# First expert's first half summed in two base tiles, z2d stored later, FFN2's rows loaded sooner, in a gated cross-attention and mixture-of-experts kernel

## The chip, the cores and the metric

The kernel runs on one core of a Trainium2 chip. The core has five engines, each with its own in-order instruction queue: TensorE (PE, matrix products), VectorE (DVE), ScalarE (ACT), GpSimd (POOL) and SyncE (SP), which here only issues DMA transfers. Transfers run on 16 DMA engines. A DMA instruction in a queue holds back everything behind it in that queue until what it waits for has happened. The metric is the device time of one execution in microseconds: 1840.61 us, median of 3 runs (1840.03 to 1844.49).

## The reference

There are B = 4 batches of 2048 tokens with 512 features, all in float32. Each batch has a context of 128 rows.

```python
n = layernorm(x)                                  # no affine
Q, K, V = n @ Wq + bq, ctx @ Wk + bk, ctx @ Wv + bv
attn = softmax(Q @ K.T) / sqrt(512)
x = x + tanh(g_x) * (attn @ V)
n = layernorm(x)
e = argmax(mean_tokens(n) @ Wr + br)              # one expert of 8 for each batch
h = relu(n @ W1[e] + b1[e])                       # 512 -> 2048
x = x + tanh(g_f) * (h @ W2[e] + b2[e])           # 2048 -> 512
```

## The kernel before

**Strassen products.** The two feed-forward products (FFN1 and FFN2) use the seven-product form of a 2 x 2 block product (as Winograd arranged it), FFN1 on two levels (7 outer groups of 7 inner products), FFN2 on one. This needs sums of blocks on both sides. The left sums of FFN1 are made from the normalised tokens in `z_prepare` (tiles z1 to z7, each with 7 places). The right sums are sums of the expert's weights. They are the same for all tokens of a batch and are called staging here.

**Staging.** An expert has two halves (`fh` 0 and 1) of its 2048 hidden features. For each half, `stage_w1` does two 128-row chunks `pc` of four outer blocks. It loads the four blocks with four inner blocks each (1 MB) from HBM into places 1 to 4 of a tile `base` ([128, 4, 7, 128]), makes three outer sums in a tile `tt` ([128, 3, 7, 128]) with `outer_sums` and the three inner sums of each outer block with `inner_sums`, all on POOL, four subtractions a call. The finished tiles are stored to HBM (W1d: one tensor for the four base blocks, one for the three tt blocks). `stage_w2` does the same for W2, on one level, in two chunks `kp`, in the same `base` buffer, and stores the four sums to W2d. `base` and `tt` have one buffer each (`stp`, one buffer). A store is not issued where its data is made: `later` queues it, and `settle` issues it some steps later, so that SP need not stand at it.

**Weights into PE.** `fetch` loads staged blocks from W1d, raw or summed blocks from W2 and W2d, into a ring of `NW` = 6 tiles `w` of 0.5 MB, in the order in which PE uses them. Before the change it asks `staged_upto` whether the whole half has been staged. FFN1's group i has a tile A (inner products 6, 1, 2, 7) and a tile B (3, 4, 5), and its last three products run inside the next group.

**Attention.** Tokens come in 16 blocks of 512. Each block is a generator, `attention`: load x and xT, statistics, scores, softmax, weighted values, statistics, store x1d (the first residual sum), normalise in place on ACT, transpose on PE, sum for routing, store z2d. The first nine blocks (numbered 0 to 8; 0 to 3 are batch 0) run in the head, a loop of steps in which every live generator emits one piece; block i starts at step `skew` x i. The tuple `AT_ONCE` gives how many steps a block waits at each of its lags. When block 1 ends, `z_prepare(0, 0)` joins the loop, and when block 3 ends, `first_expert`: `route` (mean, product with Wr, arg max; SP then reads the expert's number), then staging. The loop ends when blocks 0 to 7 are done and the first half's weights are staged. Then the main loop goes through batches, pairs of token blocks and halves: `ffn1`, then `ffn2`. `tick` emits the remaining attention and staging pieces between PE's products at rates set by `PACE`. The order on each engine is thus written by the program, not by a scheduler.

**FFN2.** `ffn2` has two half-passes `cp`, with 7 products of 3.45 us each. Product m3 accumulates in the bank that the sum of m5 is read from. That sum adds to the residual rows `xr`, which DVE has to have in SBUF: `load(cp)` reads them from x1d (`fh` 0) or y1d (`fh` 1), after the first product of the half-pass; they are written back to y1d or to the output. `xr1` and `xr0` have one buffer each.

**What is queued where.** All transfers of the head, of the ring and of staging are on SP's queue. x, x1d and z2d of the later attention blocks are on ACT's queue. Each transfer takes one of eight completion counters in turn, and so waits for the transfer eight places before it in program order. The lines of the profile that matter: L204 scores, L245 weighted values, L263 normalise, L278 transposes, L259 and L287 stores of x1d and z2d, L446 staging sums, L481 and L512 loads of W1 and W2, L471 stores of staged tiles, L563, L570 and L576 ring loads, L591 feed-forward products, L646, L662 and L666 z's load, second-level and first-level sums, L834 to L853 the xr rows.

Of the kernel before, what the change touches and what calls it, by code (L numbers as in the profile page):

```python
# [18 lines left out]
P = 128  # L19
# [70 lines left out]
def flamingo(tc, ctx, x, xT, cxT, g_x, g_f, WqT, Wk, Wv, bqk, bv, Wr, br, W1, b1, W2, b2, out):  # L90
# [52 lines left out]
    for b in range(B):  # L143
# [8 lines left out]
        for fh in range(2):  # L152
            for lo, n in ((0, 4), (4, 3)):
                t = dram.tile([P, n, 2, 7, P], F32, name=f"W1d_{b}{fh}{lo}")
                W1d.update({(b, fh, lo + i): (t, i) for i in range(n)})
            W2d[b, fh] = dram.tile([P, 2, 4, 2, Q], F32, name=f"W2d_{b}{fh}")
# [11 lines left out]
    def attention(b, blk, pools):  # L168
# [104 lines left out]
        for kc in range(KC + 1):  # L273
# [12 lines left out]
            yield  # L286
        queue.dma_start(z2d[b, blk], zT)  # L287
# [9 lines left out]
    AT_ONCE, LATER = (4, 2, 3, 7, 4, 5, 6), (2, 1, 3, 6, 3, 3, 8)  # L297
# [10 lines left out]
    if True:  # L308
# [7 lines left out]
        nc.sync.dma_start(w["k"], Wk)  # L316
# [137 lines left out]
    stores = []  # L454
    LOAD, AGE = (10, 6), 3

    def later(dst, src):

        stores.append([AGE, dst, src])

    def flush():
        for _, dst, src in stores:
            nc.sync.dma_start(dst, src)
        stores.clear()

    def older():
        for x in stores:
            x[0] -= 1
        while stores and stores[0][0] < 0:
            _, dst, src = stores.pop(0)  # L470
            nc.sync.dma_start(dst, src)  # L471

    def settle(n):
        for _ in range(n):
            older()
            yield

    def stage_w1(b, fh, eng):
        def load(pc):
            t = stp.tile([P, 4, 7, P], F32, tag="base", name="base")  # L480
            nc.sync.dma_start(  # L481
                t[:, :, 1:5, :],
                W1[bass.ds(expert[b][0], 1), fh, pc].rearrange("e p o i c -> p (e o) i c"),
            )
            return t

        flush()
        base = load(0)
        yield from settle(LOAD[b > 0])
        for pc in range(2):  # L490
            tt = stp.tile([P, 3, 7, P], F32, tag="tt", name="tt")
            for _ in outer_sums(
                eng, *(t[:, i, 1:5, :] for t, n in ((base, 4), (tt, 3)) for i in range(n))
            ):
                yield from settle(1)
            for src, lo in ((base, 0), (tt, 4)):
                for _ in inner_sums(eng, src):
                    yield from settle(1)
                later(W1d[b, fh, lo][0][:, :, pc], src)
            if pc == 0:  # L500
                yield from settle(1)
                base = load(1)
                yield from settle(LOAD[b > 0])
        yield from settle(AGE + 1)

    def stage_w2(b, fh, eng):
        for kp in range(2):
            flush()
            t = stp.tile([P, 4, 7, P], F32, tag="base", name="base2").rearrange(
                "p o i c -> p (o i c)"  # L510
            ).rearrange("p (o c) -> p o c", o=7)
            nc.sync.dma_start(  # L512
                t[:, 0:4, :],
                W2[bass.ds(expert[b][0], 1), fh, kp].rearrange("e p o k c -> p (e o) (k c)"),
            )
            yield from settle(LOAD[b > 0])
            for _ in outer_sums(eng, *(t[:, i, :] for i in range(7))):
                yield from settle(1)
            later(W2d[b, fh][:, kp].rearrange("p o k c -> p o (k c)"), t[:, 3:7, :])
            yield from settle(AGE + 1)  # L520
        flush()

    def stage(b, eng):
        for fh in range(2):
            yield from stage_w1(b, fh, eng)
            flush()
            staged_upto[0] += 1
            yield from stage_w2(b, fh, eng)
            staged_upto[0] += 1
# [6 lines left out]
    Wt, items, staged_upto = {}, [], [0]  # L536
# [14 lines left out]
    def fetch(freed=0):  # L551

        ring["freed"] += freed
        while ring["issued"] < min(ring["freed"] + NW, len(items)):
            st, kind, i = items[ring["issued"]]
            b, fh = st // (2 * NF), st % 2
            if 4 * b + 2 * fh + (kind == "2") >= staged_upto[0]:
                return
# [83 lines left out]
    def z_prepare(b, blk):  # L642
# [22 lines left out]
        def level1(o, l, r, op):  # L665
            nc.vector.tensor_tensor(z[o][:, 0:4, :], z[l][:, 0:4, :], z[r][:, 0:4, :], op)  # L666
# [30 lines left out]
    def s4(cp):  # L697
        hsum(h[12], h[12], h["s2"], ALU.subtract, cp)

    def ffn1(b, blk, fh):  # L700
# [46 lines left out]
        def group(i):  # L747
# [13 lines left out]
            def copied(v):  # L761
# [4 lines left out]
                t22 = s7p.tile([P, 2, Q], F32, tag="s722", name="s722")  # L766
# [13 lines left out]
            def summed(j, a, v):  # L780
# [6 lines left out]
                else:  # L787
                    c = cp_.tile([P, 2, Q], F32, tag="cg", name="cg", bufs=2)
# [12 lines left out]
        for i in range(8):  # L801
            cur = group(i) if i < 7 else None
            for k, (who, m) in enumerate((
# [8 lines left out]
                if i == 7 and k == 3:  # L812
                    s3(0)
            fetch((cur is not None) + (last is not None))
# [4 lines left out]
    def ffn2(b, blk, fh, half):  # L819
# [6 lines left out]
        xr, s7 = {}, {}  # L826

        def tokens(t, i, cp):
            return t[b, 2 * blk + i][:, 2 * cp : 2 * cp + 2, :]

        def load(cp):
            for i in (1, 0):
                xr[cp, i] = xrp.tile([P, 2, H], F32, tag=f"xr{i}", name="xr")
                nc.sync.dma_start(xr[cp, i], tokens(y1d if fh else x1d, i, cp))  # L834
# [7 lines left out]
        def store(cp, i):  # L842
# [4 lines left out]
            else:  # L847
                nc.sync.dma_start(tokens(y1d, i, cp), xr[cp, i])
# [32 lines left out]
        load(0)  # L881
        yield
        for cp in range(2):
# [4 lines left out]
            cur[6]()  # L888
            bias(cp, 1)
            yield  # L890
# [18 lines left out]
            if cp == 0:  # L909
                cur = group(1)  # L910
                load(1)
# [13 lines left out]
    def first_expert():  # L925
        yield from route(0, ps_k, "pk")
        yield from stage_w1(0, 0, nc.gpsimd)
        flush()
        staged_upto[0] += 1
        fetch()  # L930
        bias2_load(0)
        fetched[0] = 1
        yield from stage_w2(0, 0, nc.gpsimd)
        staged_upto[0] += 1
        yield from stage_w1(0, 1, nc.gpsimd)
        flush()
        staged_upto[0] += 1
        yield from stage_w2(0, 1, nc.gpsimd)
        staged_upto[0] += 1
# [3 lines left out]
    skew = 14  # L943
    step = 0
    while any(g is not None for g in streams[:-1]) or not fetched[0] or prep is not None:
        for i, g in enumerate(streams):
            if g is not None and step >= skew * i and next(g, StopIteration) is StopIteration:
# [3 lines left out]
                if i == 1:  # L951
                    prep = z_prepare(0, 0)
# [13 lines left out]
        if work is not None and next(work, StopIteration) is StopIteration:  # L966
            work = None
# [39 lines left out]
    PACE = {"slow": (0.6, 0.7, 0.7), "staged": (1.4, 0.7, 0.5, 0.5)}  # L1007
# [71 lines left out]
```

## Time and profile before

| What | Value |
|---|---|
| median of 3 runs | 1840.61 us |
| profiled execution | 1841.68 us, span 1839.9 us |
| mean granted PE clock | 0.966 |
| PE busy | 1713.2 us (93%) |
| DVE, ACT, POOL busy | 1025.3, 583.0, 679.3 us |
| DMA | 483.08 MB, 262 GB/s over the span |
| first weight load of the first expert issued | 149.56 us |
| first FFN1 product on PE | 221.26 us |
| first FFN2 product | 270.98 us |
| first product of the second half's FFN1 | 354.74 us |

The page divides the span in 40 slices of 46 us; a digit is the busy share of a slice in tenths, PEclk the clock that PE was granted. A row of waits names the engine and line that waited, what ended the wait, the sum in us, the number of times and the longest. A row of a timeline has the start, the duration, the engine, line and operation, output and inputs, and in brackets how long the engine had been idle and what ended it. SPq is SP's queue issuing a transfer; its duration is that of the issue, not of the transfer. Line numbers are those of the kernel before.

### The profile page before, as it was taken

The page shows a single profiled execution, that of the slowest core. Times are in us where ns is not written, and L with a number is a line of the kernel's source. Part 1 is how long each engine was busy: PE and PEld are TensorE (multiplying, and loading weights), DVE is VectorE, ACT ScalarE, POOL GpSimd, SP SyncE. Part 2 cuts the span into 40 slices and gives each one's busy share as a digit, 9 for nine tenths or more (in the row PEclk, how much of TensorE's full clock was granted, in tenths as well). Part 3 has the DMA queues.
Part 4 walks back from the last instruction along what each step waited for, and adds up shares of the span by engine and source line. Part 5 has one row for each costly group of instructions (what it writes and reads, how often), then busy time and mean ns, then how long its engine had stood idle before and what let it go on. Part 6 is the DMA issues. An engine that isn't in the chain of part 4 may idle for free.

```text
span 1839.9 us, 22357 instructions
## 1 busy us (share of the span) xinstructions
PE 1713.2 (93%) x7894; PEld 1448.4 (79%) x7894; DVE 1025.3 (56%) x1636; ACT 583.0 (32%) x1277; POOL 679.3 (37%) x616
## 2 busy tenths in 40 slices
PE   7977497899999999998999989999999999999998
PEld 5554286687878888787888878788888888888887
DVE  3586165466564866656464745465545564555453
ACT  1244250250523324161333315050505050505150
POOL 0136374285632393146510573266201510151010
PEclk9997698999999999999999999999999999999999
DMA  6485878799897888788867787879675757575754
GB/s 257 172 320 224 307 252 309 280 334 367 283 362 287 302 307 336 240 292 303 333 218 241 253 303 250 286 261 367 219 224 173 264 174 225 173 267 170 228 171 169
DMA packets 186589, 483.08 MB, mean 263 GB/s; under 512 B 13680, under 2 KB 42352, under 8 KB 173808
## 3 DMA queue, kind: packets, MB, share of 16 engines
q1 hardware_dynamic: 182592, 459.36, 71.2%
q10 hardware_dynamic: 3888, 22.31, 3.0%
q8 instruction: 63, 1.03, 0.2%
q14 instruction: 46, 0.38, 0.1%
HBM read 344.78 MB, written 136.84 MB: 262 GB/s over the span
## 4 chain that ended last, share of the span: by engine, by line
PE 70%; DMA 15%; DVE 8%; POOL 3%; issue 2%; ACT 1%; SPq 1%; ACTq 0%; DVEq 0%; POOLq 0%
PE Y L591 28%; PE X L591 18%; PE Q L591 17%; DMA z<-z2d 3%; PE psc L204 3%; DMA w<-W2d 2%; DMA base<-in_W_dram 2%; PE pav L245 2%; POOL base L446 2%; DVE xr L853 2%; DVE z L666 1%; DMA W2d<-base 1%; DMA W1d<-tt 1%; DMA out_dram<-xr 1%; POOL tt L446 1%
## 5 line engine op out<-in xcount | busy, mean ns | idle before, releaser
L591 PE MATMUL Y<-z,w 128*128 128x256 f32 x1344 | 334.5, 382 | 5.1 <-DVE c L785 2.2
L591 PEld LDWEIGHTS Y<-z,w 128*128 128x128 f32 x1344 | 251.7, 190 | 48.8 <-issue 5.9
L610 ACT COPY Y<-X 128x512 f32<-128x512 f32 x144 | 82.3, 571 | 563.8 <-PE X L591 563.4
L715 ACT ACTIVATE h<-c,b1T 128x256 f32<-128x256 f32 x512 | 229.7, 501 | 73.6 <-DVE c L731 33.0
L446 POOL TENSOR_TENSOR base<-base 128x512 f32<-128x512 f32 x144 | 190.7, 1333 | 147.6 <-DMA base<-in_W_dram 142.4
L591 PE MATMUL Q<-w,h 128*128 128x256 f32 x1024 | 238.1, 386 | 7.1 <-DMA w<-W2d 7.1
L591 PE MATMUL Y<-w,s 128*128 128x256 f32 x1024 | 235.3, 383 | 2.2 <-DMA w<-W2d 2.2
L591 PE MATMUL X<-w,h 128*128 128x256 f32 x1024 | 232.5, 379 | 0.0
L591 PE MATMUL X<-z,w 128*128 128x256 f32 x896 | 216.3, 380 | 14.5 <-DMA w<-W1d 14.5
L591 PEld LDWEIGHTS Q<-w,h 128*128 128x128 f32 x1024 | 197.7, 194 | 38.5 <-issue 10.8
L662 POOL TENSOR_TENSOR z<-z 128x256 f32<-128x256 f32 x224 | 188.4, 865 | 97.0 <-DMA z<-z2d 54.8
L591 PEld LDWEIGHTS Y<-w,s 128*128 128x128 f32 x1024 | 196.6, 192 | 32.4 <-issue 5.3
L591 PEld LDWEIGHTS X<-w,h 128*128 128x128 f32 x1024 | 194.3, 190 | 29.7 <-issue 3.3
L591 PE MATMUL Q<-z,w 128*128 128x256 f32 x896 | 216.5, 381 | 0.6
L591 PEld LDWEIGHTS X<-z,w 128*128 128x128 f32 x896 | 170.1, 191 | 38.6 <-issue 15.4
L591 PEld LDWEIGHTS Q<-z,w 128*128 128x128 f32 x896 | 169.6, 191 | 24.7 <-PE Y L591 1.0
L734 POOL TENSOR_TENSOR r<-r,cg 128x512 f32<-128x512 f32 x32 | 40.6, 1269 | 370.8 <-DVE cg L789 370.8
L591 PE MATMUL Y<-w,h 128*128 128x256 f32 x512 | 126.3, 401 | 24.7 <-DVE xr L853 24.7
L591 PEld LDWEIGHTS Y<-w,h 128*128 128x128 f32 x512 | 101.9, 202 | 45.4 <-DVE xr L853 29.8
L195 POOL TENSOR_TENSOR rstd<-ve,mhalf 128x4 f32<-128x4 f32 x32 | 32.8, 1025 | 230.6 <-DVE ve L194 218.3
L853 DVE SCALAR_TENSOR_TENSOR xr<-X,gf,xr 128x512 f32<-128x512 f32 x32 | 24.0, 751 | 159.5 <-PE X L591 121.6
L838 DVE TENSOR_TENSOR xr<-xr,b2g 128x1024 f32<-128x1024 f32 x32 | 40.4, 1261 | 99.6 <-DMA xr<-x1d 80.7
(120 smaller groups left out, 1983.3 us busy)
## 6 DMA issues: line engine op xcount, KB each, us to landing
w<-W2d SPq DMA_DIRECT2D x128, 512.0 KB, 5.4
w<-W1d SPq DMA_DIRECT2D x112, 512.0 KB, 5.7
w<-in_W_dram SPq DMA_DIRECT2D x96, 512.0 KB, 6.4
w<-W1d SPq DMA_DIRECT2D x112, 384.0 KB, 5.0
base<-in_W_dram SPq DMA_DIRECT2D x32, 1024.0 KB, 7.7
W1d<-base SPq DMA_DIRECT2D x16, 1792.0 KB, 8.8
W1d<-tt SPq DMA_DIRECT2D x16, 1344.0 KB, 10.9
xT<-in_xT_dram SPq DMA_DIRECT2D x16, 1024.0 KB, 10.6
```

The source lines that it names most:

```text
L195: nc.gpsimd.tensor_tensor(rstd, ve, mhalf, ALU.pow)
L204: nc.tensor.matmul(psc[:, t, :], lhsT=xTt[:, kc, t * P : (t + 1) * P], rhs=Mb[:, kc, :], start=kc == 0, stop=kc == KC - 1,)
L245: nc.tensor.matmul(pav[t], lhsT=pT[:, t * P : (t + 1) * P], rhs=Vb, start=True, stop=True)
L446: eng.tensor_tensor(o, l, r, ALU.subtract)
L591: nc.tensor.matmul(bank[:, c, :], lhsT=left(k, c), rhs=right(k, c), start=fresh and c == 0 and k == 0, stop=c == 1 and k == ks - 1, skip_g ...
L610: nc.scalar.copy(t["Y"], t["X"])
L662: nc.gpsimd.tensor_tensor(a[o], a[l], a[r], op)
L666: nc.vector.tensor_tensor(z[o][:, 0:4, :], z[l][:, 0:4, :], z[r][:, 0:4, :], op)
L715: nc.scalar.activation(h[ij][:, v, 2 * m + c, :], src[:, c, :], AF.Relu, bias=b1T[:, f + c : f + c + 1],)
L734: eng.tensor_tensor(r[j], r[j], v, ALU.add)
L838: nc.vector.tensor_tensor(xr[cp, i], xr[cp, i], b2g.unsqueeze(1).to_broadcast([P, 2, H]), ALU.add)
L853: nc.vector.scalar_tensor_tensor(o, v, gf, o, ALU.mult, ALU.add)
```

## The change

1. `stage_first` takes the place of `stage_w1` for the first expert's first half. Both chunks are loaded at once: chunk 0 into `base`, chunk 1 into two buffers of the x pool of the head. Inner sums come first, on pairs of outer blocks (256 elements a row); then outer sums over all seven places at once (896 elements). The four base blocks are stored in two parts, the first of them right after its inner sums. The first W2 chunk is loaded at the end of it.
2. `stage_w1`, for all other halves: inner sums first, then outer sums over seven places; tt is stored after three of the four outer sums; the second chunk is loaded in the next turn of the loop.
3. `fetch` asks for single blocks (`made`, filled as stores are issued) rather than whole halves, and raw W2 blocks may be loaded at any time. In the head it runs at every step.
4. The store of z2d has a lag of 3 steps of its own, the lags around xT's load are 3 and 8 rather than 5 and 6, and `skew` is 13 rather than 14.
5. The first-level sums of the first `z_prepare` run on POOL rather than DVE.
6. Wk is loaded in two halves.
7. `xr` of the first half-pass is loaded in FFN1 after group 5; `xr0` has two buffers; the bias is added one piece later. `s722` moves to the buffers of `cg`, which become three.
8. `PACE` of the first expert's rest is 1.1 rather than 1.4.

```diff
-            for lo, n in ((0, 4), (4, 3)):
+            for lo, n in ((0, 4), (4, 3)) if b + fh else ((0, 2), (2, 2), (4, 3)):
                 t = dram.tile([P, n, 2, 7, P], F32, name=f"W1d_{b}{fh}{lo}")
...
+        yield from wait(lag[7])
         queue.dma_start(z2d[b, blk], zT)
...
-    AT_ONCE, LATER = (4, 2, 3, 7, 4, 5, 6), (2, 1, 3, 6, 3, 3, 8)
+    AT_ONCE, LATER = (4, 2, 3, 7, 4, 3, 8, 3), (2, 1, 3, 6, 3, 3, 8, 0)
...
-        nc.sync.dma_start(w["k"], Wk)
+        for c in range(2):
+            nc.sync.dma_start(w["k"][:, :, c * Q : (c + 1) * Q], Wk[:, :, c * Q : (c + 1) * Q])
...
+    def stage_first(eng, x0):
+        base = stp.tile([P, 4, 7, P], F32, tag="base", name="base")
+        blocks = [[base[:, 0:2], base[:, 2:4]], []]
+        for _ in range(2):
+            t = x0.tile([P, 4, H], F32, tag="x", name="base")
+            blocks[1].append(
...
+        base_load(base, 0, 0, 0)
+        yield
+        for i in range(2):
+            base_load(blocks[1][i], 0, 0, 1, slice(2 * i, 2 * i + 2))
+            yield
+        yield from settle(LOAD[0] - 3)
...
+        for i in range(2):
+            for pc in range(2):
+                for _ in inner_sums(eng, blocks[pc][i]):
+                    yield from settle(1)
+                if i == 0:
+                    late(0, pc)
+        for pc in range(2):
+            tt = stp.tile([P, 3, 7, P], F32, tag="tt", name="tt")
+            outer = [blocks[pc][i // 2][:, i % 2] for i in range(4)] + [tt[:, i] for i in range(3)]
+            for i, _ in enumerate(outer_sums(eng, *outer)):
+                yield from settle(1)
+                if i == 2:
+                    later(W1d[0, 0, 4][0][:, :, pc], tt, *((0, 0, 4 + j) for j in range(3 * pc)))
+            late(1, pc)
+        nonlocal base2
+        base2 = base2_load(0, 0, 0)
+        yield from settle(AGE + 1)
+
+    def stage_w1(b, fh, eng):
+        for pc in range(2):
+            base = stp.tile([P, 4, 7, P], F32, tag="base", name="base")
+            tt = stp.tile([P, 3, 7, P], F32, tag="tt", name="tt")
+            base_load(base, b, fh, pc)
+            yield from settle(LOAD[b > 0])
+            for _ in inner_sums(eng, base):
+                yield from settle(1)
+            for i, _ in enumerate(
+                outer_sums(eng, *(t[:, i] for t, n in ((base, 4), (tt, 3)) for i in range(n)))
             ):
-                yield from settle(1)
...
+                yield from settle(2)
+                if i == 2:
+                    later(W1d[b, fh, 4][0][:, :, pc], tt, *((b, fh, 4 + j) for j in range(3 * pc)))
+            later(W1d[b, fh, 0][0][:, :, pc], base, *((b, fh, j) for j in range(4 * pc)))
+            yield from settle(AGE + 1)
...
-            if 4 * b + 2 * fh + (kind == "2") >= staged_upto[0]:
+            need = (b, fh, "2" if kind == "2" else RIGHT[ORDER[i]])
+            if need not in made and not (kind == "2" and RIGHT[ORDER2[i % 7]] < 3):
                 return
...
-            nc.vector.tensor_tensor(z[o][:, 0:4, :], z[l][:, 0:4, :], z[r][:, 0:4, :], op)
+            eng.tensor_tensor(z[o][:, 0:4, :], z[l][:, 0:4, :], z[r][:, 0:4, :], op)
...
+    def sums_load(b, blk, fh, cp):
+        for i in (1, 0):
+            xr[cp, i] = xrp.tile([P, 2, H], F32, tag=f"xr{i}", name="xr", bufs=2 - i)
+            nc.sync.dma_start(xr[cp, i], tokens(y1d if fh else x1d, b, blk, i, cp))
...
-                t22 = s7p.tile([P, 2, Q], F32, tag="s722", name="s722")
+                t22 = cp_.tile([P, 2, Q], F32, tag="cg", name="s722", bufs=3)
...
-                    c = cp_.tile([P, 2, Q], F32, tag="cg", name="cg", bufs=2)
+                    c = cp_.tile([P, 2, Q], F32, tag="cg", name="cg", bufs=3)
...
+            if i == 5:
+                sums_load(b, blk, fh, 0)
             fetch((cur is not None) + (last is not None))
...
-        load(0)
         yield
...
             cur[6]()
+            yield
             bias(cp, 1)
-            yield
...
-                load(1)
+                sums_load(b, blk, fh, 1)
...
-        yield from stage_w1(0, 0, nc.gpsimd)
-        flush()
-        staged_upto[0] += 1
-        fetch()
+        yield from stage_first(nc.gpsimd, three[0])
+        fetched[0] = 1
         bias2_load(0)
-        fetched[0] = 1
-        yield from stage_w2(0, 0, nc.gpsimd)
+        yield from stage_w2(0, 0, nc.gpsimd, base2)
...
-    skew = 14
+    skew = 13
...
-                    prep = z_prepare(0, 0)
+                    prep = z_prepare(0, 0, nc.gpsimd)
...
-    PACE = {"slow": (0.6, 0.7, 0.7), "staged": (1.4, 0.7, 0.5, 0.5)}
+    PACE = {"slow": (0.6, 0.7, 0.7), "staged": (1.1, 0.7, 0.5, 0.5)}
```

## The prediction

> **What bounds the kernel now.** I read the slices of the page first, then TensorE's waits, then the timelines of SP, POOL and PE around the worst slices. The page:
>
> ```profile
> span 1839.9 us, 22357 instructions
> ...
> PE 1713.2 (93%) x7894; PEld 1448.4 (79%) x7894; DVE 1025.3 (56%) x1636; ACT 583.0 (32%) x1277; POOL 679.3 (37%) x616
> ...
> PE   7977497899999999998999989999999999999998
> ...
> PEclk9997698999999999999999999999999999999999
> DMA  6485878799897888788867787879675757575754
> ```
>
> Each digit is 46 us. PE is short only in the first eight slices; DMA is dense there too. Of PE's 127 us idle, about 66 lie before its first feed-forward matmul at 221.3 us and about 61 after it. From the table of 92 us stretches, an undisturbed stage keeps PE busy 91.9 of 92 us. The waits of PE:
>
> ```profile
> PE Y L591 <- DVE xr L853: 24.7, 13, 4.9
> PE X L591 <- DMA w<-W1d: 14.5, 1, 14.5
> PE pt L278 <- ACT x L263: 10.8, 4, 10.1
> PE psc L204 <- DMA xT<-in_xT_dram: 10.6, 2, 6.2
> ```
>
> The first row is FFN2 waiting for residual rows (13 times in 32 half-passes). The next two are the wait for the first expert's weights. SP's timeline shows why they come late:
>
> ```profile
> 149.56 0.68 SPq L481 DMA_DIRECT2D base<-in_W_dram  x1
> ...
> 157.00 0.33 SPq L287 DMA_DIRECT2D z2d<-zT  x1
> 157.45 0.36 SPq L259 DMA_DIRECT2D x1d<-x  x1
> 175.62 0.32 SPq L287 DMA_DIRECT2D z2d<-zT  x1
> 176.05 0.60 SPq L471 DMA_DIRECT2D W1d<-base  x1
> 184.45 0.61 SPq L481 DMA_DIRECT2D base<-in_W_dram  x1
> ...
> 210.31 0.51 SPq L471 DMA_DIRECT2D W1d<-tt  x1
> ```
>
> SP stands from 157.8 to 175.6 us at a z2d store; then the second weight load waits until the one base tile has been stored (184.45). POOL therefore starts its second half only at 194.94, after 15.63 us idle, and the first matmul comes at 221.26:
>
> ```profile
> 221.26 2.05 PE L591 MATMUL X<-z,w 128*128 128x256 f32 x4 [14.50 <-DMA w<-W1d]
> ...
> 302.48 3.78 PE L204 MATMUL psc<-M,xT 128*128 128x128 f32 x16 [6.15 <-DMA xT<-in_xT_dram]
> 309.13 3.78 PE L591 MATMUL Y<-w,h 128*128 128x256 f32 x8 [2.87 <-DVE xr L853]
> ```
>
> A stall also costs clock: those 16 score matmuls take 3.78 us against 1.95 when warm.
>
> **What the Trainium skill says.** GPSIMD Engine Reference, section "Elementwise — side-by-side cycle accounting", gives about 2.6 cycles an element for a two-input add; the trace agrees (POOL: 512 elements in 1.27 us, 256 in 0.72). DMA: Bandwidth & Descriptors, "Two DMAs through the same engine are not ordered", has the issuing engine wait on the first DMA's semaphore before it issues a dependent one: that is SP's stand before 184.45, and all behind it in SP's queue waits too. TensorE: Matmul & The Clock Gate, "What's actually happening": idling for a window halves the clock until the array has been busy about as long; the 3.78 against 1.95 agrees. SBUF — State Buffer, "Who interferes with whom": a DVE instruction with two SBUF inputs and GpSimd's reads contend; the z sums take 0.72 us each in the head but 0.865 on average, which fits.
>
> **The change part by part.** I call the issue of the first weight load T=0 (149.56 now).
>
> *Head up to T=0.* z's four first-level sums go from DVE (1.22 us each, 4.9 in all) to POOL. By 512 in 1.27 and 256 in 0.72, POOL takes 0.17 + 2.15 ns an element: 2.4 us each, 9.5 in all. DVE was busy 16.1 of 18 and 18.2 of 20 us between 92 and 130, POOL 5.5 of 20; POOL's reciprocal roots (1.02 us) queue behind these sums, and DVE and ACT wait for them. Skew 13 starts each block earlier; the z2d lag of 3 steps gives that back for route, but SP waits less at z2d and xT is issued before route rather than after (PE waited 4.46 us for it at 162.6). The split of Wk gains nothing: keys wait for bqk_t at 11.67; wq is issued some 4 us later and ends about when it is needed. I take -5, bounds -12 and +5.
>
> *T=0 to the first matmul, 71.7 us now.* Both halves are loaded at once. POOL starts at 11.7 as now. Inner sums of the first two blocks of both halves: 8 x 0.72 plus two roots and a late third load, done at 20. The second of two 0.9 MB stores is issued then and, between 1.0 MB in 6.6 and 1.8 MB in 8.8, lands at 26.5; weights issued, landed at 32 (5.7 a load). But stream 7's x1d store stands behind them in SP's queue: issued 28, landed 38 (10.2), and ACT's normalisation, the transposes and the zero matmuls took 9.5 us (197.3 to 206.8). First matmul at 47.5: -24 (bounds 40, were x1d not in the way, and 60, if z2d of the sixth block holds SP as it does now). POOL's sum is equal (16 x 1.27 + 8 x 1.02 = 28.5 against 16 x 0.72 + 8 x 2.10 = 28.3; 896 elements being 2.10 by the same line), but it runs without the 15.6 us gap.
>
> *FFN1's first pass, 49.7 us now.* Outer sums end on POOL at 34 and 43; tt's second store is issued at 43, lands at 52, third weight tile at 58; SP then waits for the base store (59) and for the W2 store (65) before it issues the tile of the last three products: landed at 71. Groups 1 to 3 run 47.5 to 66 at 6.05 us each, the fourth stands 5 us, the later ones 1 or 2 more. End at 99: 51.5 us.
>
> *FFN2's first pass, 83.8 us now.* Now three W2 tiles are ahead; the fourth is queued behind tt's and base's stores of the second half and the load that waits for them. Weights loaded at 84.5, landed 92, POOL's sums (5.1 + 8.4 and two r sums) to 109, store landed 118, fourth tile 125; needed at 109.5. A new stall of some 15 us (bounds 5, if the stores land as fast as the quickest now, and 22). Against it fall the xr waits (2.87 at 309, and 5.53 at 340.9, where DVE stood 8.56 us for xr; with the clock 13) and the xT wait (6.15 + 1.8: xT now stands ahead in the queue). From 125: 11 products x 3.45 + 8 for attention's matmuls + 5 left = 176. So the second half's FFN1 starts at 176 instead of 205.2: -29 in all since T=0.
>
> *Later FFN2.* xr's first rows are loaded during FFN1, a dozen us before use; the work that hides them is two FFN1 groups. First-half waits after 400 us: 3.41, 0.59, 0.89, 1.51, 3.76, 0.71, 1.39, 0.71 = 13.0 plus the slow matmuls after them (6.71 for 3.45 at 428.7, 5.25 at 1162, the rest 0.1 to 0.3 each), 6.5: -19. Second halves (0.58, 1.09, 4.91, 2.25 = 8.8, plus 3.3): the xr0 load no longer waits for its own store, issued 3.45 us after xr1's, so up to 2.5 of each goes, with most of the clock: -8. SP's cost: the loads only move. Of this 27 I keep 21, as the w<-W2d waits (2.64 at 516, 4.46 at 832) come nearer.
>
> *Shared cg buffers; longer POOL sums.* Nothing, while POOL frees the oldest of three within a group (6 us); if not, see the last rival.
>
> *Density.* From 150 to 460 us DMA's share is about 0.82; the same bytes in 35 us less make 0.92. I add 4 us back.
>
> Sum against the profiled execution's 1841.7 us (span 1839.9): -5 - 29 - 21 + 4 = -51, so 1790.7. The median of the runs shown is 1.1 lower: 1789.6, say 1790.
>
> **The rivals.** *The head goes better*: the fourth-tile stall is half as long (-8), T=0 comes 12 earlier instead of 5 (-7) and density costs nothing (-4): -19, 1771. For it: SP's order loses many stands. Against: DMA is at 1.04 already at 280 to 300. *The head's gain is eaten*: PE starts early and starves behind SP's stores, the second half's FFN1 still comes 205 us after T=0: then -5 - 21 = -26, 1815. For it: weights still pass through HBM and one base tile from the second half on. *The rows are hidden already or other waits step in*: xr's waits turn into w<-W2d waits: -5 - 29 + 4 = -30, 1811 (as would be if the rows were hidden from the start). Against it: DVE stood 72.1 us for xr<-x1d after 360 us with the weights there. *Slower*: s722 shares three buffers with cg, and POOL's r sums, which free them, stand behind four outer sums of 2.1 us (8.4 in a row, where they now pass between ops of at most 1.3). The place is FFN1 wherever an expert is staged: 14 such bursts after the first half (seven halves, two tiles each). If each holds DVE and then PE for 4.4 us and 1.8 us of slow clock follow, 14 x 6.2 = 87 us are lost and the time is 1877; it decides from 51 / 14 = 3.6 us lost in every burst. For it: r<-r,cg already takes 1.76 us at one of its lines against 1.27 at the other, so POOL is held up there. Against: PE's longest wait for such a sum (c at L785) is 1.24 us now, and cg alone gets one buffer more.
>
> **How the numbers follow.** Forecast 0.54 (own range 1775 to 1804), better head 0.18, eaten 0.15, other waits 0.08, slower 0.05. 1790 is the likeliest. 1762 to 1818 leaves about 2 in 10 out. Within 0.3%, 5.5 us, which is about what these runs can tell from no change, is a case halfway to slower: 0.02. Slower 0.04, faster 0.94.
>
> **What would show it.** First feed-forward matmul near 192 us; POOL without the 15 us gap between the two halves; a w wait of 10 to 20 us in the first FFN2; second FFN1 start near 320; the xr row of PE's waits under 6 us; no c or cg row above 3 us. Wrong if the first FFN1 stands for tens of us on w<-W1d, if T=0 comes after 155, or if w<-W2d waits grow by what xr loses.

## The result, and the profile after

The changed kernel takes 1826.2 us (median of 5, 1825.0 to 1831.2); the kernel before, run beside it, took 1840.6 us. The ratio is 0.9924, with a 95% interval of 0.9896 to 0.9952: a gain of 14 us. The prediction said 51, and 1826 lies above its range. The profiled execution took 1828.6 us, 13.1 us less than that of before.

Line numbers from here on are those of the kernel that a view is of. In the changed kernel L631 is the feed-forward product, L650 FFN1's first copy, L898 the sum with xr, L448 a staging sum, L466 a store of a staged tile, L478 and L487 are the loads of W1 and W2, L603, L610 and L616 the ring loads, L749 the load of the rows. T=0 is, as in the prediction, the issue of the first weight load.

The page of the changed kernel, slices of 45.7 us:

```profile
span 1826.8 us, 22361 instructions
...
PE   7977588989999998998999989999999999999998
...
PEclk9988798989999999999999999999999999999999
```

The fifth slice, in which PE waited for the first weights, is one digit better (5 for 4, clock 7 for 6), and so are the seventh and the eighth. But the sixth, which FFN1's first pass now fills in large part, shows 8 for 9, and so does the ninth, from 365 us on, with a clock of 8 for 9. A gain is made early and partly given back. The starts of the passes on PE say by how much (us; the last line is the profiled execution's time):

| | before | after | difference |
|---|---|---|---|
| first weight load issued | 149.56 | 152.57 | +3.0 |
| FFN1, first pass | 221.26 | 193.28 | -28.0 |
| FFN2, first pass | 270.98 | 261.18 | -9.8 |
| FFN1, second half | 354.74 | 334.80 | -19.9 |
| FFN2, second half | 400.84 | 382.53 | -18.3 |
| third FFN1 | 464.14 | 454.54 | -9.6 |
| tenth FFN1 | 1191.38 | 1180.65 | -10.7 |
| the execution's time | 1841.68 | 1828.62 | -13.1 |

Two stretches of this table lose: FFN1's first pass (67.9 us for 49.7) and FFN2 in the second half (72.0 for 63.3). PE's waits after, to be set beside those shown of before (sum, times, longest):

```profile
PE pav L245 <- DVE x L249: 17.7, 8, 4.2
PE X L631 <- DMA w<-in_W_dram: 15.0, 2, 10.9
PE Y L631 <- DVE xr L898: 13.9, 10, 6.7
PE Y L631 <- ACT Y L650: 11.0, 1, 11.0
PE Q L631 <- DMA w<-W2d: 9.2, 2, 5.9
PE Y L631 <- DMA w<-W1d: 4.4, 1, 4.4
```

The 14.5 us for w<-W1d and the 10.6 for xT are gone, and xr fell from 24.7 to 13.9. In their place stand two waits which before did not have, for raw W2 tiles (15.0) and for ACT (11.0 in one piece), and 2 us more for this row of w<-W2d. The first row is attention's own (3.9 us before): 10.6 of its 17.7 us lie in the head, ahead of the first FFN1.

**What stands behind them.** ACT's timeline, after:

```profile
202.71 2.93 ACT L263 ACTIVATE x<-x,shift,rstd 128x512 f32<-128x512 f32 x4 [10.33 <-DMA x1d<-x]
```

PE's timeline, after, the three long waits of the first two passes:

```profile
206.17 2.08 PE L631 MATMUL Y<-z,w 128*128 128x256 f32 x4 [11.00 <-ACT Y L650]
229.08 1.14 PE L631 MATMUL Y<-z,w 128*128 128x256 f32 x4 [4.37 <-DMA w<-W1d]
282.64 6.40 PE L631 MATMUL X<-w,h 128*128 128x256 f32 x16 [10.94 <-DMA w<-in_W_dram]
```

ACT normalises token block 8 in place, and so has to wait until its x1d store has landed. This stands in ACT's queue in front of FFN1's first copy, and PE can't go on without the copy. SP's timeline says why the store was late, and why tiles are missing at 229 and 282:

```profile
185.18 0.52 SPq L466 DMA_DIRECT2D W1d<-base  x1
193.48 0.34 SPq L487 DMA_DIRECT2D base<-in_W_dram  x1
193.92 0.38 SPq L259 DMA_DIRECT2D x1d<-x  x1
...
214.98 0.38 SPq L466 DMA_DIRECT2D W2d<-base  x1
223.10 0.34 SPq L487 DMA_DIRECT2D base<-in_W_dram  x1
223.54 1.69 SPq L616 DMA_DIRECT2D w<-W1d  x3
...
262.18 0.56 SPq L466 DMA_DIRECT2D W1d<-base  x1
275.23 0.61 SPq L478 DMA_DIRECT2D base<-in_W_dram  x1
277.31 0.39 SPq L603 DMA_DIRECT2D w<-in_W_dram  x1
```

Three times the same picture: the one base tile is stored, the next load into it stands in SP's queue until the store has landed (7.8, 7.7 and 12.5 us of silence), and what was queued behind, the x1d store or ring tiles, goes out in the moment after. It goes on so through the whole of staging. Late in it the rows of FFN2 stand behind such a load, and the longest wait with the label xr (6.7 us) comes of that:

```profile
1053.12 0.56 SPq L466 DMA_DIRECT2D W1d<-base  x1
1063.22 0.56 SPq L478 DMA_DIRECT2D base<-in_W_dram  x1
...
1065.19 1.04 SPq L749 DMA_DIRECT2D xr<-y1d  x2
```

```profile
1081.93 6.12 PE L631 MATMUL Y<-w,h 128*128 128x256 f32 x16 [6.68 <-DVE xr L898]
```

DVE stood 15.3 us for these rows, to 1075.41. What SP waited for, in the same columns as PE's waits, in the kernel before (L481 and L512 are the loads of W1 and W2):

```profile
SPq L481 <- DMA W1d<-base: 46.2, 8, 9.2
SPq L512 <- DMA W1d<-base: 18.7, 4, 8.0
```

And after (L478 and L487):

```profile
SPq L487 <- DMA W1d<-base: 72.0, 8, 12.3
SPq L478 <- DMA W1d<-base: 71.9, 7, 15.7
```

64.9 us of standing behind W1's base stores have become 143.9. (Such a sum isn't time lost by itself: in the same queue the stands at the rows' loads behind their own stores fell from 94.3 us to 16.2. It depends on what stands behind.) A store goes out four steps after `later` has been called for it. Before, base was handed over after its inner sums; its store went out with the last of tt's four sums, and the next load came two steps later (W1's second chunk) or five (W2). In all fourteen such gaps after the first half SP issued one to six other transfers between the store and the load. The new order hands base over last, and the load comes in the step after the store: in nine of the fourteen gaps nothing stands between the two.

### The profile page after: what moved, and what is told of

Read it like the earlier page. It is cut to its first block, busy times and chain, and to the rows that moved or that the text cites. A ratio compares the mean times of both kernels' runs of the same rounds, so it can differ in the third digit from the quotient of the medians.

```text
span 1826.8 us, 22361 instructions
## 1 busy us (share of the span) xinstructions
PE 1705.0 (93%) x7893; PEld 1438.4 (79%) x7894; DVE 1020.7 (56%) x1632; ACT 581.7 (32%) x1277; POOL 669.3 (37%) x564
## 4 chain that ended last, share of the span: by engine, by line
PE 69%; DMA 13%; DVE 10%; issue 3%; POOL 3%; SPq 1%; ACT 0%; DVEq 0%; POOLq 0%; ACTq 0%
PE Y L631 27%; PE Q L631 18%; PE X L631 17%; DMA W1d<-base 3%; DMA z<-z2d 2%; PE pav L245 2%; DMA w<-in_W_dram 2%; DMA W2d<-base 1%; DVE st L189 1%; POOL base L448 1%; DVE xr L898 1%; PE psc L204 1%; DVE h L726 1%; POOL tt L448 1%; DVE z L706 1%
## 5 line engine op out<-in xcount | busy, mean ns | idle before, releaser
L631 PE MATMUL Y<-z,w 128*128 128x256 f32 x1344 | 334.5, 383 | 21.3 <-ACT Y L650 11.0
L448 POOL TENSOR_TENSOR base<-base 128x512 f32<-128x512 f32 (+2 forms) x152 | 203.0, 1343 | 313.1 <-DMA base<-in_W_dram 308.4
L631 PEld LDWEIGHTS Y<-z,w 128*128 128x128 f32 x1344 | 251.6, 190 | 67.3 <-ACT Y L650 14.2
L631 PE MATMUL X<-w,h 128*128 128x256 f32 x1024 | 238.4, 385 | 15.0 <-DMA w<-in_W_dram 15.0
L631 PE MATMUL Q<-w,h 128*128 128x256 f32 x1024 | 236.5, 384 | 9.2 <-DMA w<-W2d 9.2
L650 ACT COPY Y<-X 128x512 f32<-128x512 f32 x144 | 82.2, 571 | 501.2 <-PE X L631 486.4
L631 PEld LDWEIGHTS X<-w,h 128*128 128x128 f32 x1024 | 197.6, 194 | 46.1 <-DMA w<-in_W_dram 15.8
L631 PE MATMUL Y<-w,s 128*128 128x256 f32 x1024 | 232.5, 379 | 0.7 <-DVE s L726 0.7
L631 PEld LDWEIGHTS Q<-w,h 128*128 128x128 f32 x1024 | 197.1, 193 | 40.4 <-issue 13.2
L631 PEld LDWEIGHTS Y<-w,s 128*128 128x128 f32 x1024 | 194.2, 190 | 29.9 <-issue 2.9
L631 PE MATMUL Q<-z,w 128*128 128x256 f32 x896 | 216.8, 382 | 0.8
L631 PE MATMUL X<-z,w 128*128 128x256 f32 x896 | 217.0, 380 | 0.5 <-DMA w<-W1d 0.5
L631 PEld LDWEIGHTS Q<-z,w 128*128 128x128 f32 x896 | 170.0, 191 | 25.7 <-issue 1.6
L631 PEld LDWEIGHTS X<-z,w 128*128 128x128 f32 x896 | 169.8, 191 | 24.2 <-PE X L631 0.9
L785 POOL TENSOR_TENSOR r<-r,cg 128x512 f32<-128x512 f32 x32 | 40.6, 1270 | 373.2 <-DVE cg L840 373.2
L898 DVE SCALAR_TENSOR_TENSOR xr<-X,gf,xr 128x512 f32<-128x512 f32 x32 | 24.0, 750 | 240.8 <-PE X L631 117.9
L631 PE MATMUL Y<-w,h 128*128 128x256 f32 x512 | 123.3, 395 | 14.0 <-DVE xr L898 13.9
L631 PEld LDWEIGHTS Y<-w,h 128*128 128x128 f32 x512 | 100.1, 198 | 34.1 <-DVE xr L898 19.1
L245 PE MATMUL pav<-V,pT 128*128 128x512 f32 x128 | 72.0, 675 | 30.9 <-DVE x L249 17.7
## 6 DMA issues: line engine op xcount, KB each, us to landing
W1d<-base SPq DMA_DIRECT2D x14, 1792.0 KB, 11.3
```

The source lines that it names most:

```text
L245: nc.tensor.matmul(pav[t], lhsT=pT[:, t * P : (t + 1) * P], rhs=Vb, start=True, stop=True)
L448: eng.tensor_tensor(o, l, r, ALU.subtract)
L631: nc.tensor.matmul(bank[:, c, :], lhsT=left(k, c), rhs=right(k, c), start=fresh and c == 0 and k == 0, stop=c == 1 and k == ks - 1, skip_g ...
L650: nc.scalar.copy(t["Y"], t["X"])
L785: eng.tensor_tensor(r[j], r[j], v, ALU.add)
L898: nc.vector.scalar_tensor_tensor(o, v, gf, o, ALU.mult, ALU.add)
```

## The experiments

The theory after this result (S): the missing gain is lost where SP stands at a load behind the store of the same base tile, because ring tiles and x1d stores stand behind it. Its rivals: the rows were worth less than counted (Q), and the DMA engines are full, so that nothing would land sooner (D). All ratios are against the kernel before, run beside each kernel. A change of kernel moves some stretches between single profiles as well: in eight profiles with the changed head, T=0 came between 152.6 and 155.6 us, so that smaller differences in T=0 say nothing, while the time from T=0 to the first FFN1 was 40.6 to 41.1 us in all of them.

### What the rows are worth

The changed kernel with the rows loaded as before:

```diff
-            if i == 5:
-                sums_load(b, blk, fh, 0)
...
         cur[1]()
         s2(0)
+        sums_load(b, blk, fh, 0)
         yield
```

(with one buffer for xr0 and the bias piece back in its place)

> The changed kernel with the residual rows loaded as before: after the first product of each half-pass, one buffer for xr0, bias one piece earlier. Theory R (the prediction): the rows' earlier load is worth 27 us less what other waits take, so this costs 15 to 27 us more than the changed kernel, 1841 to 1853, and the xr row of PE's waits goes from 13.9 back to 25 us. Theory Q (most of what the profile calls a wait for xr after 400 us is DVE held by z's load or by its own queue): only the half-passes of fh 0 and the second half-passes change, 2 to 10 us more, 1828 to 1836.

1838.0 us, ratio 0.9977 (0.9965 to 0.9989): 12 us more than the changed kernel by the medians, 10 by the ratios. That lies between the ranges of the two theories; the xr row of PE's waits is 24.2 us, as R had it. And the other way round, part 7 alone put into the kernel before:

> The kernel before with only the rows' earlier load, the second xr0 buffer, the later bias and the shared cg buffers. Theory R: 20 to 27 us faster than before plus the waits at 309 and 341 us (13), 1800 to 1815. Theory Q: 5 to 15 us faster, 1826 to 1836, most of it in the first FFN2 pass.

1832.8 us, ratio 0.9948 (0.9925 to 0.9971): 9 us less than before, as Q had it, though only some 3 of them fall before the second half's FFN1. Both sides agree on 9 to 12 us, not the 21 of the prediction; by the intervals of the ratios, 5 to 14 us would fit both. DVE's timeline in the changed kernel shows a part of what the label xr had hidden:

```profile
415.61 3.62 DVE L706 TENSOR_TENSOR z<-z,z 128x1024 f32<-128x1024 f32 x3 [3.31 <-DMA z<-z2d]
...
420.16 0.75 DVE L898 SCALAR_TENSOR_TENSOR xr<-Y,gf,xr 128x512 f32<-128x512 f32 x1
```

PE waits at 420.96 for "DVE xr", and DVE had its rows: the same half-pass's earlier sums with xr had run from 408.71 on. It was held by the first-level sums of the next block's z, and they by z's load. In the kernel before it is the same at 428.7 (z's sums at 422.55, after 1.72 us of waiting for z2d). `z_prepare` runs in every FFN2 pass with `fh` 1 up to the last block, and in each of these seven passes three of z's sums, 3.6 us together, stand just ahead of the sum with xr; in three of the seven they had themselves waited for z2d (0.6 to 1.7 us). These seven first waits are among the thirteen that the row counts: 9.2 of its 24.7 us before, and 6.2 of the 13.9 after. An earlier load of rows can't remove what z's sums hold. Most of the rest of the 13.9 us is the one wait at 1081.93, which is for rows, held by SP.

### SP's stands in staging

Six empty turns between the base store of W1 and the next load, in the changed kernel:

```diff
             later(W1d[b, fh, 0][0][:, :, pc], base, *((b, fh, j) for j in range(4 * pc)))
-            yield from settle(AGE + 1)
+            yield from settle(AGE + 1 + 6)
```

> The changed kernel with six more steps between the store of a W1 base tile and the load of the next chunk into its buffer, so that SP issues ring tiles while the store lands. Theory S (the load stands in SP's queue right behind the store and holds the ring tiles): the wait of 10.9 us at 282 and those of 3.3 and 4.1 at 389 and 402 go, the first FFN2 pass falls from 73.6 to about 60 and the second from 72 to about 63, total 10 to 25 us faster than the changed kernel. Rival D (DMA is saturated there, tiles come late whatever the order): waits move, total within 4 us.

1801.4 us, ratio 0.9794 (0.9769 to 0.9819): 24 us less than the changed kernel, by a delay. SP's waits of this kernel:

```profile
SPq L478 <- DMA W1d<-base: 15.4, 3, 9.4
SPq L487 <- DMA W1d<-base: 12.1, 2, 7.9
```

143.9 us have become 27.5. The first FFN2 pass takes 65.2 us instead of 73.6, the second 61.3 instead of 72.0. PE's wait for raw W2 tiles falls from 15.0 to 4.3 us, and the wait for rows at 1081.93 is 0.2 at the same place. Theory D falls here: the tiles did land sooner.

Is it the order of the sums that does it? Part 2's order undone, all else as changed:

```diff
+        for pc in range(2):
+            for _ in outer_sums(eng, *(t[:, i, 1:5, :] ...)):
+                yield from settle(1)
+            for src, lo, n in ((base, 0, 4), (tt, 4, 3)):
+                for _ in inner_sums(eng, src):
+                    yield from settle(1)
+                later(W1d[b, fh, lo][0][:, :, pc], src, ...)
+            if pc == 0:
+                yield from settle(1)
+                base = load(1)
```

> Part 2 undone: outer sums first, base stored four inner sums ahead of the next load, all else as changed. Theory S expects most of what the six turns gave: 1800 to 1812 us, and FFN2's second pass 60 to 65 us (72.0 with the change). The rival, that the six turns helped by slowing staging down and not by what stands in SP's queue, expects no gain from the old order: 1820 to 1832.

1812.5 us, ratio 0.9840 (0.9809 to 0.9871): 15 us less than with the new order, and SP's standing behind W1's base stores is 62.2 us, as in the kernel before. That is just outside what S expected; the second FFN2 pass, 67.0 us, gives back only half. So the new order costs this kernel some 15 us, and the rest of the six turns' gain goes beyond the old order. (The old order also stores tt last and has one step fewer after each outer sum.)

Are such turns good for any kernel? The same six turns put into the kernel before:

```diff
             if pc == 0:
-                yield from settle(1)
+                yield from settle(1 + 6)
                 base = load(1)
...
-        yield from settle(AGE + 1)
+        yield from settle(AGE + 1 + 6)
```

> The kernel before, with six more turns ahead of the second chunk's W1 load and after W1's staging. There the base tile's store is issued some four sums ahead of the load already. Theory S expects little: within 6 us of before, 1835 to 1847. The rival (six more turns are good whatever the order of the stores) expects a gain like that in the changed kernel: 1812 to 1828.

1853.6 us, ratio 1.0064 (1.0029 to 1.0100): 12 us slower. SP's standing behind W1's base stores fell there too, from 64.9 to 4.3 us, yet the second FFN1 pass grew from 46.1 to 59.9 us, with waits for w<-W1d of 3.0 and 4.0 us at 353 and 372, which fits staging that comes too late. Both theories missed the size, and the rival's sign is wrong. So removing stands isn't a gain by itself; the turns have a price, and here it was the larger.

### FFN1's first pass

The x1d store ahead of the first W2 load:

```diff
-        base2 = base2_load(0, 0, 0)
-        yield from settle(AGE + 1)
+        yield from settle(1)
+        base2 = base2_load(0, 0, 0)
+        yield from settle(AGE)
```

> The changed kernel with one SP instruction moved: the load of the first W2 chunk is emitted one step later, so that block 8's x1d store stands ahead of it instead of behind it. If block 8's store is what stops ACT at 192 us, its 10.3 us wait falls to 2 to 5 and the first FFN1 pass from 67.9 to about 60 us. Theory S (SP's chain of stores and loads sets the end of both first passes): the tile waits at 229 and 282 us grow by as much, and the total stays within 3 us of the changed kernel. Theory P (each stall adds): 6 to 9 us faster than the changed kernel.

1825.1 us, ratio 0.9911 (0.9890 to 0.9932): no gain that can be told, within S's 3 us. PE's timeline in this kernel:

```profile
202.82 2.08 PE L632 MATMUL Y<-z,w 128*128 128x256 f32 x4 [4.27 <-ACT Y L651]
229.62 2.07 PE L632 MATMUL Y<-z,w 128*128 128x256 f32 x4 [8.28 <-DMA w<-W1d]
```

The wait for ACT fell from 11.0 to 4.3 us, so the cause was named rightly. The wait at 282 did not grow, as S expected, but fell to 5.5 us. But the wait for the next W1d tile grew from 4.4 to 8.3: that tile stands behind the W2 load, whose time is set by its own store (SP silent to 223.59). So both have to go. The x1d store ahead, and six turns after W2's stores as well as W1's:

```diff
                 *((b, fh, "2") for _ in range(kp))
             )
-            yield from settle(AGE + 1)
+            yield from settle(AGE + 1 + 6)
```

> The six turns also after each W2 chunk's store, and the x1d store ahead of the first W2 load. The W2 load of the first half's second chunk stood 7.7 us in SP's queue behind its own store (223.10 after), in front of three tiles of FFN1. Theory S (loads standing behind their stores hold the ring) expects FFN1's first pass to fall from 67.9 us to 52 to 58, and 1783 to 1795 us. Rival D (the DMA engines are full, and a tile that is issued sooner lands no sooner) expects 64 to 68 us for the pass and the time of the version with the six turns in W1 alone, 1798 to 1806.

1798.1 us, ratio 0.9758 (0.9731 to 0.9785). The first pass takes 58.2 us and the first FFN2 58.3, and the second half starts at 310.9, 24 us sooner than with the change. That is as S had it, but the time is not: it lies at the edge of what D expected, 3 us above S. One later FFN1 pass, 618.5 to 680.2, takes 61.6 us where the kernel before took 44.5, with a wait of 13.48 us for w<-W1d at 648.65; in the first pass there is one of 4.26. The tile at 648 is one of the second expert: SP issued no ring load from 619.1 to 642.6 us, but two stores and two loads of staging, with its stands between them. Staging came too late there, as it seems to have done in the kernel before with its turns. With the turns after W2's stores for the first expert only (`AGE + 1 + 6 * (b == 0)`):

> The x1d store ahead, six turns after W1's stores everywhere, and after W2's stores for the first expert only. Theory S (and that the 13.5 us wait for a W1d tile at 648 with the six turns everywhere came of staging the second expert too late) expects the first two passes as short as there (58 and 58 us), no wait for W1d over 5 us after 400, and 1778 to 1790 us. The rival, that DMA and POOL are full and any gain early is paid back later, expects 1794 to 1803.

1784.2 us (1778.2 to 1793.5), ratio 0.9696 (0.9659 to 0.9733): 59 us less than the kernel before, and 42 less than the changed one. It is the best version here, within S's range; only the wait at 646, 5.3 us, is a little over the 5 that S allowed. Of PE's waits in it, w<-W1d has 8.9 us (two times) and xr 8.1 (seven times). The twelve longest rows hold neither raw W2 tiles nor w<-W2d any more, and the mean clock is 0.983 (0.973 with the change). In this kernel the rows' worth can be taken again, with most of SP's stands behind W1's base stores out of the way (22.8 us are left): rows as before the change, all else as in the last one.

> The first of these versions with the residual rows loaded as before the change: what the rows are worth once SP's stands are gone. Theory R (the rows were worth the 21 us that the prediction kept, and the stands in SP's queue ate half) expects 18 to 25 us more than with the rows early. Theory Q (most of the waits that bear the label xr were z's sums on DVE, which the rows do not touch) expects 7 to 14 us more.

1796.4 us, ratio 0.9746 (0.9720 to 0.9773): 12 us more (9 by the ratios; 1 to 18 would fit), as with the stands and near the 9 of the kernel before. This is what Q expected: the stands did not eat half of the rows' worth.

### The head, and what starts FFN1

The first weight load (T=0) came 3.0 us later, not 5 sooner; in four profiles with the old head it came between 149.6 and 151.5. Part 5 undone (`prep = z_prepare(0, 0)`, on DVE):

> Part 5 undone: the first z sums on DVE again. Theory H (these sums hold POOL's reciprocal roots back, and so the attention blocks and the first weight load) expects the first weight load at 144 to 149.5 us instead of 152.57, and 1818 to 1823 us. The rival (z's load is late in any case and DVE then stands at it) expects the load at 151 to 155 and 1824 to 1830.

T=0 at 152.73; 1831.2 us, ratio 0.9937 (0.9899 to 0.9976), no difference from the change that can be told, so H falls. With the sums on POOL, they wait there 11.28 us for z2d and hold a reciprocal root to 126.92; on DVE they hold it to 126.76. z's load sets both. The z2d lag undone (last of `AT_ONCE` 0 instead of 3):

> The changed kernel without the three steps ahead of the z2d store (part 4). Theory L (routing starts where block 3's generator ends, so the three steps put the first weight load back) expects that load at 146.5 to 150.5 us instead of 152.57 and 1819 to 1824 us. The rival (SP then stands at each z2d store, as in the kernel before) expects the load at 151 to 156 and 1825 to 1835.

T=0 at 155.07, within the spread; 1834.9 us, ratio 0.9956 (0.9940 to 0.9973): not sooner, as the rival had it, and the lag is worth some 6 us where it stands (the two intervals just overlap). In the best version it is worth more:

> Both of the two versions above in one. If the effects add: 3 to 6 us less than the first of them, 1773 to 1786. If SP stands at the z2d stores: no gain or 2 to 8 us more.

1808.2 us, ratio 0.9816 (0.9788 to 0.9843), 24 us more than with the lag, far outside both cases; its first FFN1 starts at 207.8 instead of 194.7, and 9.5 us of waiting for a DVE memset come just ahead of it. The spacing of the blocks leads to the same wait. `skew` 14 again:

> The changed kernel with the blocks 14 steps apart again (part 4, one third). If the closer spacing is what puts the first weight load at 152.57 (DVE has to take routing's five small operations in behind more of the neighbours' work), the load comes at 148 to 151. If it is not, it comes 1 to 4 us later than 152.57, by block 3's three steps.

1837.3 us, ratio 0.9982 (0.9969 to 0.9996): nearly all that the change had won is gone with one step of spacing. T=0 comes 3.7 us later, as the second case expected (0.6 beyond the spread), but the first FFN1 19 us later, at 212.4. POOL's timeline of this kernel:

```profile
198.91 2.09 POOL L448 TENSOR_TENSOR tt<-base 128x896 f32<-128x896 f32 x1 [4.08 <-DMA W1d<-tt]
...
207.28 1.01 POOL L195 TENSOR_TENSOR rstd<-ve,mhalf 128x4 f32<-128x4 f32 x1
```

And DVE's:

```profile
208.32 1.22 DVE L257 SCALAR_TENSOR_TENSOR shift<-mv,rstd 128x4 f32<-128x4 f32 x1 [13.47 <-POOL rstd L195]
209.54 0.27 DVE L1019 MEMSET zero<- 128x256 uint32 x1
```

Block 8's reciprocal root, 1 us long, stands on POOL behind the outer sums of the second chunk, and they behind tt's store. DVE waits 13.5 us for the root, and the memset behind it, on which PE's zero products ahead of FFN1 wait, comes at 209.5. In the changed kernel the root falls between the two chunks, at 185.11, and DVE waits 5.1 us. One step of spacing decides on which side it falls. The lags around xT's load at 5 and 6 again:

> The changed kernel with the lags around xT's load at 5 and 6 again (part 4, another third; the z2d lag stays). If these lags put the first weight load back, it comes at 147 to 151. If not, at 152 to 155.

T=0 at 155.96, a little above both ranges; 1826.9 us, ratio 0.9930 (0.9907 to 0.9953), as with the change. And parts 4 and 5 undone together:

> Parts 4 and 5 undone together: skew 14, the old lags, no z2d lag, first z sums on DVE. If these parts as a whole moved the first weight load from 149.56 to 152.57, it returns to 148.5 to 150.5. If the split of Wk or the loads of W2 tiles in the head did, it stays at 152 to 154.

T=0 at 150.08, and the first FFN1 at 213.2; 1838.9 us, ratio 0.9992 (0.9977 to 1.0007). So it is the head's new schedule that moved T=0, and not the split of Wk. No single part of it, undone alone, brought T=0 back. Where the time goes can be told: from block 3's last zT to the first weight load it took 13.8 to 14.0 us in the eight profiles with the changed head, and 9.3 in the four with the old one (this run, the kernel before, and its versions with the rows and with the turns). It is 11.9 without the lag, 11.4 with the old spacing, 12.7 with the old lags and 13.2 with the sums on DVE. Block 3 itself ended at 138.8 to 141.7 with the changed head and at 140.3 to 142.2 with the old one, so whether the blocks end sooner can't be told. Why routing takes 4.5 us longer to come to its turn stays open.

## Why the prediction was wrong

Its direction was right, and the late W2 tile that it foresaw came. Its sum was 38 us too good:

| Step | predicted | measured |
|---|---|---|
| head up to T=0 | -5 | +3.0 |
| T=0 to the first matmul | -24.2 | -31.0 |
| FFN1's first pass | +1.8 | +18.2 |
| FFN2's first pass | -6.8 | -10.1 |
| later FFN2, with density | -17 | +6.9 |

**"Head up to T=0"** failed by 8 us. The 5 us that the spacing and the shorter stands at z2d were to give did not reach the load: what block 3 gained, if anything, is within the spread, and routing took 4.5 us longer to come to its turn.

**"T=0 to the first matmul, 71.7 us now"** came out at 40.7 instead of 47.5, by the path that it named. Stream 7's x1d store was issued 24.7 us after T=0 (28 predicted), ACT's normalisation of that block began at 33.1 (38, the store's landing), PE waited for it, and the first product came 7.6 us later (9.5):

```profile
186.50 0.48 PE L278 MATMUL pt<-ident,x 128*128 128x128 f32 x1 [8.35 <-ACT x L263]
```

What the step did not see is how near another path was. With skew 14 this stretch is 56 us, without the lag 55, with parts 4 and 5 undone 63: then PE waits 8.3 to 9.5 us for the memset behind block 8's reciprocal root, which stands behind POOL's sums. The step named POOL's roots, but only as 1 us each. With the old head the rest of the change buys 8.5 us here, and the head's schedule the other 22; the new head without the two base tiles was not run. That the step came near is in part luck.

**"FFN1's first pass"** failed by 16 us. It followed the ring tiles through SP's queue and left out what SP does for attention: block 8's x1d store, on which ACT stands ahead of FFN1's own copies (11.0 us). The prediction had a wait of this kind before its eyes: its third row of PE's waits, the 10.1 us for ACT, is block 7's normalisation behind its x1d store, and not, as it says there, a wait for the first expert's weights. The runs with x1d ahead and turns after W2's stores bring the pass to 58 us; 4 us of each wait remain there.

**"FFN2's first pass"** held. A tile was late by 10.9 us (15 predicted, bounds 5 and 22), with the slow products after it, and the pass took 73.6 us where 77 was predicted.

**"Later FFN2"** failed twice. Its 21 us for the rows took every xr wait for a wait for rows. The row names the instruction that PE waits for, not what held DVE: in seven of the waits it was z's sums, and one of those for rows stayed, because the second half-pass's rows stood behind staging in SP's queue. The runs show 9 to 12 us for the whole kernel, and 3 to 5 of these fall between T=0 and the second half's FFN1 (by the profiles of the two runs on the rows), where this step did not count them. And the step let part 2 go through the later stages at no cost. It had found, for the first half, that a tile stands behind "tt's and base's stores of the second half and the load that waits for them", and did not ask how often that comes again: it comes at most of the chunks. Undoing the order is worth 15 us, of which 4 to 7 fall before the second half's FFN1 (counted from the start and from T=0); in the profiled executions 7 of 12 fall after it. So some 12 to 17 us of the rows and 7 to 11 of the order are missing there, 19 to 28 together, and the sum was off by 24. This split is an estimate from the starts of the passes in single profiles; the two were not undone together in one kernel. Nor were parts 3, 6 and 8 undone alone. Of these the slower `PACE` of the first expert's rest (part 8) could have a share in what is lost after 335 us, and the 4 us for density can't be told apart either.

**The rivals.** "The head's gain is eaten" (1815) comes nearest in kind: weights pass through one base tile, and PE starves behind SP's stores. But it expected the second half's FFN1 to start as late after T=0 as before, 205 us, and it came after 182: the loss lay in FFN1's first pass and after 335 us. That xr's waits turn into w<-W2d waits did not show: these are 9.2 us for 9.3 before. The slower case, POOL's long sums holding cg, did not show: no c or cg row stands among PE's waits above 0.7 us. POOL's sums of 896 elements took 2.09 us in the median, as worked out, but it was a reciprocal root that they held.

## What to carry to other kernels

When one buffer is stored and loaded again, count the instructions between the store's issue and the load's in the same queue: with none, the queue stood here for the store's whole landing, and everything behind it, in every turn of the loop and not only in the one that you look at. Put the load later or the urgent transfers ahead of it, but only where the next consumer has time to spare: six turns of delay won 24 us in one kernel and cost 12 in another. And before you price a wait by its label, look at the timeline of the engine named and see what it was doing.

## What was not expected of the hardware

- The store of a whole base tile (1.75 MB) took 11.3 us from issue to landing in the median with the change (14 stores), 8.8 before (16), while tt's went the other way, 7.5 for 10.9. SP stood up to 15.7 us for one. Why is not shown.
- The place of a 1 us operation in POOL's queue, one step of the program away, decided some 15 us of when FFN1 starts: 56 us after T=0 with skew 14, 40.6 to 41.1 in the eight profiles with the changed head.
- With fewer stalls the clock was higher: the mean granted clock of the profiled executions went 0.966, 0.973, 0.983 from before over the change to the best version, and PE's busy time from 1713 over 1705 to 1693 us, for the same products.
